# Spike counts summed by TensorE, two gather tiles, an eighth chunk held, and output tiles taken from the row buffers

## Chip, cores and metric

One core of a Trainium2 chip runs the whole program. The metric is the device time in microseconds (us) of one execution, as the median over many runs. 1 us is 1000 ns.

## What is computed

The inputs are 1024 sequences of 50 item numbers (`r_seq`), their lengths, and a table of 100001 embedding rows of 128 floats, whose row 0 counts as zero. For each time step the reference takes the running mean of the embeddings, normalises it over the batch, feeds it to a leaky integrate-and-fire neuron per sequence and feature, and averages the spikes over the 50 steps. The scores are the product of that average with the whole table: 1024 x 100001 floats, 409.6 MB.

```python
emb = emb_table.at[0].set(0.0)
e = emb[seq]
prefix = jnp.cumsum(e, axis=1)
denom = jnp.minimum(t_idx[None, :], lengths[:, None])
uF = prefix / denom[:, :, None]
y = (uF - uF.mean(0)) * lax.rsqrt(uF.var(0) + BN_EPS) * gamma + beta
def step(v, x):
    v = v + (x - v) / TAU
    spike = atan_spike(v - V_TH)
    v = v - spike * V_TH
    return v, spike
_, spikes = lax.scan(step, v0, x_seq)      # 50 steps
scores = spikes.mean(axis=0) @ emb.T
```

## The kernel before

The program has two stages. Instructions stand in every engine's queue in the order in which the Python code issues them (line 49 switches any reordering off), so a wait in a queue holds all that is behind it.

**Stage one, the 50 steps** (loop of line 271). Everything is held transposed, features on the 128 partitions and the 1024 sequences along the row, in two halves of 512. For each step POOL (GpSimd) issues 8 indirect DMAs (line 187), one for each block of 128 sequences, that fetch the embeddings of that step into a tile `e`. There are three such tiles (`gather`, line 166), and the gather of step t+1 is issued at the head of step t, so it can run ahead until it needs a tile whose readers are not done. PE (TensorE) adds the prefix sum up in PSUM: `pre[0]` and `pre[1]`, one for each half, get 8 transposing matmuls out of `e` (line 284) and a matmul each that takes out row 0 (`correct`, line 252). DVE (VectorE) then reads `pre` into `uF` (line 293), half by half, and takes batch statistics (lines 294 and 298). The second half of `uF` can't start before the last four of the 8 transposes. Still on DVE come the spikes of the step before, `s` (line 308, 1 or 0 in bf16), and five small operations that make the scale `a` (lines 310 to 316). ACT (ScalarE) makes the square root and two passes over the whole row (lines 302, 303 and 322). DVE ends the step with `negv` (line 330), the new potential `v` (line 325, in PSUM, tiles `v0` and `v1` in turn), and `count` (line 263): it adds the step's spikes to a running sum in SBUF. The next transposes stand in PE's queue directly behind `correct`, and `correct` needs `uF` of the step to be read.

At steps 42, 44 and 46, and at the end, a quarter (1024 rows) of the first chunk of the table is prepared as well (`prepare`, line 138): 8 transposes on PE into a PSUM tile `pt`, a copy on ACT that rounds to the upper part `hi` (line 132), and a subtraction on DVE for the rest, `lo` (line 136).

**Stage two, the product** (loop of line 391). The table is cut into 25 chunks of 4096 rows; the last has 1697. `AHEAD = 7` chunks are loaded at the very start on SP's queue (line 180), the others in stage two on ACT's queue, one after each chunk. The prepared quarters live in six pairs of tiles `hi` and `lo`, taken in turn (`slot`, line 105). For each of the 8 blocks of 128 sequences, PE multiplies the four quarters by the counts (`product`, line 145, two parts in two banks for each quarter), DVE and ACT in turn scale the result into an output tile `o` (lines 403 and 405; three tiles of 16 KB a partition), and SP's queue stores it (line 157, 2 MB). The four quarters of the next chunk are prepared after the third block, after the sixth, and two inside the last block (lines 409 to 414).

Of the kernel before, what the change touches and what calls it, by code (L numbers as in the profile page):

```python
# [12 lines left out]
F32 = mybir.dt.float32  # L13
BF16 = mybir.dt.bfloat16
F32R = mybir.dt.float32r
# [5 lines left out]
P = 128  # L21
BN_EPS = 1e-5
V_TH = 1.0
CH = 4096
AHEAD = 7
HALF = 1024
KQ = HALF // P
BANK = 512
# [3 lines left out]
def rec_kernel(  # L32
# [17 lines left out]

    const = ctx.enter_context(tc.tile_pool(name="const", bufs=1))
    embp = ctx.enter_context(tc.tile_pool(name="embT", bufs=1))
    rowp = ctx.enter_context(tc.tile_pool(name="rows", bufs=AHEAD - 1))


    countA = const.tile([P, P], F32R, tag="countA", name="countA")
# [9 lines left out]
    chunks = [(c0, min(CH, N - c0)) for c0 in range(0, N, CH)]  # L66
    rows = {}
    split = {}
    order = {}
    for c, (c0, w) in enumerate(chunks):  # L70
        for q in range(-(-w // HALF)):
            order[c, q] = len(order)

    def fetch(c, pool):

# [27 lines left out]
            nc.tensor.transpose(pt[:, k0 : k0 + kw], rows[c][:kw, q * KQ + k0 // P, :], ident[:kw, :kw])  # L103

    def slot(c, q):
        i = order[c, q] % 6
        pool = embp if i < 4 else embp2
        hi = pool.tile([P, HALF], F32R, tag=f"hi{i}", name=f"hi_{c}_{q}")
        lo = pool.tile([P, HALF], F32R, tag=f"lo{i}", name=f"lo_{c}_{q}")
        split[c, q] = hi, lo  # L110
        return hi, lo

    def views(c, q, pt, hi, lo):
# [18 lines left out]
        nc.scalar.copy(vh, vp)  # L132

    def lower(c, q, pt):
        vp, vh, vl = views(c, q, pt, *split[c, q])
        nc.vector.tensor_tensor(vl, vp, vh.bitcast(F32), ALU.subtract)  # L136

    def prepare(c, q, pt):
# [5 lines left out]

    def product(po, c, q, n, k0, kw):
        kw += kw % 2
        for j, part in enumerate(split[c, q]):
# [12 lines left out]
    with ExitStack() as ph:  # L160
# [2 lines left out]
        lp = ph.enter_context(tc.tile_pool(name="lif", bufs=2))  # L163
        sp = ph.enter_context(tc.tile_pool(name="stats", bufs=3))
        up = ph.enter_context(tc.tile_pool(name="uF", bufs=2))
        gp = ph.enter_context(tc.tile_pool(name="gather", bufs=3))
        accp = ph.enter_context(tc.tile_pool(name="acc", bufs=1, space=bass.MemoryType.PSUM))
        vp = ph.enter_context(tc.tile_pool(name="v", bufs=1, space=bass.MemoryType.PSUM))

# [74 lines left out]
        def only(t):  # L244

# [4 lines left out]
        def correct(t, l):  # L250
            for h in range(B // BANK):
                nc.tensor.matmul(  # L252
                    pre[h],
                    lhsT=l,
                    rhs=zT[:, h * BANK : (h + 1) * BANK],
                    start=t == 0,
                    stop=False,
                    skip_group_check=True,
                )


        def spiked(out, cs, v):
            nc.vector.scalar_tensor_tensor(out, v[:, cs], V_TH, count[:, cs], ALU.is_ge, ALU.add)  # L263
# [7 lines left out]
        for t in range(T):  # L271
            last = t == T - 1
            if t + 1 < T:
                gather(t + 1)
            e = es.pop(t)
            if last:
                s = lp.tile([P, B], BF16, tag="s", name=f"s_{t - 1}")
                nc.vector.tensor_single_scalar(s, v, V_TH, ALU.is_ge)
                nc.vector.tensor_tensor(negv, s, v, ALU.subtract)
            uF = up.tile([P, B], F32, tag="uF", name=f"uF_{t}")  # L280
            bs = sp.tile([P, B // BANK, 6], F32, tag="bs", name=f"bs_{t}")
            for h, cs in enumerate(halves):
                for k in range(0, BANK, P):
                    nc.tensor.matmul(  # L284
                        pre[h][:, k : k + P],
                        lhsT=e[:, h * BANK + k : h * BANK + k + P],
                        rhs=ident,
                        start=False,
                        stop=last,
                        is_transpose=True,  # L290
                        skip_group_check=True,
                    )
                nc.vector.scalar_tensor_tensor(uF[:, cs], rlen[:, cs], 1.0 / (t + 1), pre[h], ALU.max, ALU.mult)  # L293
# [12 lines left out]
            if t and not last:  # L306
                s = lp.tile([P, B], BF16, tag="s", name=f"s_{t - 1}")
                nc.vector.tensor_single_scalar(s, v, V_TH, ALU.is_ge)  # L308
# [12 lines left out]
            def x(cs):  # L321
                nc.scalar.activation(vt[:, cs], uF[:, cs], AF.Identity, bias=hgb[:, 1:2], scale=a)  # L322

            def step(cs):
                nc.vector.scalar_tensor_tensor(vt[:, cs], negv[:, cs], -0.5, vt[:, cs], ALU.mult, ALU.add)  # L325

            if not last:
                x(whole)
                if t:
                    nc.vector.tensor_tensor(negv, s, v, ALU.subtract)  # L330
                step(whole)
                v = vt
# [11 lines left out]
        pt = accp.tile([P, HALF], F32, tag="pt", name="pt_3")  # L344
# [18 lines left out]
        spiked(countB, slice(P, BANK), vt)  # L363
        spiked(countC, halves[1], vt)
        for q in range(1, 4):
            o = (up if q == 3 else gp).tile([P, HALF], F32, tag="uF" if q == 3 else "e", name=f"o_0_0_{q}")
            po = (accp if q % 2 == 0 else vp).tile(
                [P, HALF], F32, tag="v0" if q % 2 else "pt", name=f"po_0_0_{q}"
            )
            for k0 in range(0, HALF, BANK):  # L370
                product(po[:, k0 : k0 + BANK], 0, q, 0, k0, BANK)
            for h, cs in enumerate(halves):
                if h == 0:
                    nc.scalar.mul(o[:, cs], po[:, cs], 1.0 / T)
                else:
                    nc.vector.tensor_scalar_mul(o[:, cs], po[:, cs], 1.0 / T)
# [10 lines left out]
    def ready(c, q):  # L387
        if (c, q) in order:
            prepare(c, q, psum.tile([P, HALF], F32, tag="ps", name=f"pt_{c}_{q}"))

    for c, (c0, w) in enumerate(chunks):
        for n in range(NB):
            if c == 0 and n == 0:
                continue
            o = op.tile([P, CH], F32, tag="o", name=f"o_{c}_{n}")
            for q in range(-(-w // HALF)):
# [21 lines left out]

# [17 lines left out]
```

## Time and profile before

| what | value |
|---|---|
| median of 14 runs | 1677.32 us (1676.72 to 1678.48) |
| the profiled execution: its time | 1679.74 us |
| its span, first to last instruction | 1678.0 us |
| the rest of that time, around the span | 1.74 us |
| POOL's first and last gather | begins at 3.91 us, ends at 567.44 us |
| `uF` of the last step begins | 591.12 us |
| first store of scores issued | 600.18 us |
| busy over the span | PE 1054.0, DVE 999.3, ACT 630.7, POOL 379.2 us |
| read from and written to memory | 77.69 MB and 409.60 MB |

The span is the time from the first to the last instruction of the profiled execution. A group of instructions is a line of the kernel on one engine with one kind of operation; its row gives the busy time in all, the mean of one, and how long the engine stood idle just before it and what ended that. "remote" is put where the profile knows no sender of the signal that ended a wait. Starts of matmuls are recorded, their ends are modelled, and some records of them can be missing.

### The profile page before, as it was taken

Reading aid. Unit: us, or ns where it says so; the run is one execution under the profiler, and the core shown is the slowest. Engines: PE = TensorE matmul, PEld = TensorE weight load, DVE = VectorE, ACT = ScalarE, POOL = GpSimd, SP = SyncE. Lnnn points to the kernel's source line nnn. Section 1 sums busy time; section 2 is a strip of 40 time slices with the busy share of each in tenths; the row PEclk is TensorE's granted clock in tenths of the full one; section 3 lists DMA queues with packets and bytes.
Section 4 is the critical chain, followed back from the end, with each engine's and each line's share of the span. In section 5 each row is a group of like instructions: output and inputs, shape, how many; then the busy total and the mean of one; then the engine's idle time right before and its main releaser. Section 6 shows DMA issues by size and latency. Waiting matters only on the chain.

```text
span 1678.0 us, 12554 instructions
## 1 busy us (share of the span) xinstructions
PE 1054.0 (63%) x4434; PEld 804.0 (48%) x4434; DVE 999.3 (60%) x1211; ACT 630.7 (38%) x697; POOL 379.2 (23%) x406
## 2 busy tenths in 40 slices
PE   3223323232223378778878788777877888888886
PEld 2112212221112256666666566656666666666664
DVE  5577767777768775555555455544555555555553
ACT  2122222222223244444444344444444444444452
POOL 7666666666667300000000000000000000000000
PEclk7555555555555589999999999999999999999998
DMA  9311111111111169999999999999999999999998
GB/s 342 104 46 49 48 44 47 47 46 46 46 45 49 27 255 418 425 425 421 425 418 418 415 416 419 419 425 412 418 416 419 415 424 422 417 411 413 418 413 352
DMA packets 58411, 488.14 MB, mean 291 GB/s; under 512 B 12491, under 2 KB 13292, under 8 KB 33772
## 3 DMA queue, kind: packets, MB, share of 16 engines
q1 hardware_dynamic: 35728, 424.57, 60.1%
q0 software_dynamic: 12800, 26.24, 6.0%
q10 hardware_dynamic: 9820, 36.52, 6.0%
q8 instruction: 35, 0.57, 0.1%
q14 instruction: 28, 0.23, 0.0%
HBM read 77.69 MB, written 409.60 MB: 290 GB/s over the span
## 4 chain that ended last, share of the span: by engine, by line
DMA 49%; DVE 29%; PE 7%; another core or an unknown queue 7%; issue 4%; ACT 3%; DVEq 0%; SPq 0%; ACTq 0%; POOLq 0%
DMA scores<-o 48%; PE po L148 6%; DVE o L403 6%; DVE bs L294 4%; DVE uF L293 4%; DVE v L325 3%; DVE count L263 3%; DVE s L308 3%; DVE negv L330 2%; ACT o L405 2%; ACT v L322 1%; DVE a L316 1%; DMA e<-in_L_rec_emb_table,idx 1%; DVE mv L298 1%
## 5 line engine op out<-in xcount | busy, mean ns | idle before, releaser
L403 DVE TENSOR_SCALAR o<-po 128x1024 f32<-128x1024 f32 x390 | 462.2, 1220 | 442.9 <-DMA scores<-o 357.5
L405 ACT ACTIVATE o<-po 128x1024 f32<-128x1024 f32 (+1 forms) x390 | 385.6, 1018 | 546.6 <-DMA scores<-o 382.7
L187 POOL DMA_INDIRECT e<-in_L_rec_emb_table,idx x400 | 378.5, 946 | 187.6 <-issue 114.0
L148 PE MATMUL po<-hi,countC 128*128 128x512 f32 x784 | 332.0, 424 | 91.8 <-ACT o L405 91.1
L252 PE MATMUL pre<-zT,l 128*128 128x512 f32 x100 | 77.3, 775 | 386.3 <-DVE uF L293 313.8
L148 PE MATMUL po<-lo,countC 128*128 128x512 f32 x784 | 317.7, 406 | 0.0
L148 PE MATMUL po<-hi,countB 128*128 128x512 f32 x588 | 243.2, 414 | 32.0 <-ACT o L405 31.5
L148 PE MATMUL po<-lo,countB 128*128 128x512 f32 x588 | 235.8, 401 | 0.0
L252 PEld LDWEIGHTS pre<-zT,l 128*128 128x128 f32 x100 | 28.7, 288 | 428.2 <-issue 313.5
L148 PEld LDWEIGHTS po<-hi,countC 128*128 128x128 f32 x784 | 154.5, 197 | 154.8 <-ACT o L405 124.4
L148 PEld LDWEIGHTS po<-lo,countC 128*128 128x128 f32 x784 | 154.7, 197 | 29.3
L103 PE MATMUL pt<-ident,rows 128*128 128x128 f32 x782 | 113.5, 292 | 74.2 <-ACT o L405 68.0
L302 ACT ACTIVATE r<-mv,eps 128x1 f32<-128x1 f32 x50 | 14.7, 295 | 386.6 <-DVE mv L298 229.9
L136 DVE TENSOR_TENSOR lo<-pt,hi 128x1024 fp32r<-128x1024 f32 x98 | 117.4, 1216 | 63.3 <-ACT hi L132 63.3
L148 PEld LDWEIGHTS po<-hi,countB 128*128 128x128 f32 x588 | 115.5, 196 | 69.8 <-ACT o L405 41.5
L103 PEld LDWEIGHTS pt<-ident,rows 128*128 128x128 f32 x782 | 96.6, 150 | 98.6 <-ACT o L405 83.6
L293 DVE SCALAR_TENSOR_TENSOR uF<-rlen,pre 128x512 f32<-128x512 f32 x100 | 67.8, 678 | 122.8 <-remote 105.5
L148 PEld LDWEIGHTS po<-lo,countB 128*128 128x128 f32 x588 | 115.2, 196 | 22.7
L132 ACT CAST hi<-pt 128x1024 fp32r<-128x1024 f32 x98 | 98.9, 1010 | 55.9 <-PE pt L103 42.8
L284 PE MATMUL pre<-ident,e 128*128 128x128 f32 x400 | 98.6, 419 | 11.0 <-DMA e<-in_L_rec_emb_table,idx 8.4
L284 PEld LDWEIGHTS pre<-ident,e 128*128 128x128 f32 x400 | 83.5, 220 | 24.3 <-issue 12.4
L148 PE MATMUL po<-hi,countA 128*128 128x512 f32 x194 | 76.0, 392 | 1.6 <-ACT o L405 1.1
(61 smaller groups left out, 678.5 us busy)
## 6 DMA issues: line engine op xcount, KB each, us to landing
scores<-o SPq DMA_DIRECT2D x190, 2048.0 KB
rows<-in_L_rec_emb_table ACTq DMA_DIRECT2D x17, 2048.0 KB
rows<-in_L_rec_emb_table SPq DMA_DIRECT2D x7, 2048.0 KB
scores<-o SPq DMA_DIRECT2D x8, 848.5 KB
e<-in_L_rec_emb_table,idx POOLq DMA_INDIRECT x400
scores<-o SPq DMA_DIRECT2D x2, 1024.0 KB
scores<-o SPq DMA_DIRECT2D x3, 512.0 KB
scores<-o SPq DMA_DIRECT2D x2, 256.0 KB
```

The lines of the kernel that those rows point to most:

```text
L103: nc.tensor.transpose(pt[:, k0 : k0 + kw], rows[c][:kw, q * KQ + k0 // P, :], ident[:kw, :kw])
L132: nc.scalar.copy(vh, vp)
L136: nc.vector.tensor_tensor(vl, vp, vh.bitcast(F32), ALU.subtract)
L148: nc.tensor.matmul(po[:, :kw], lhsT=counts[n], rhs=part[:, k0 : k0 + kw], start=j == 0, stop=j == 1,)
L187: nc.gpsimd.indirect_dma_start(out=es[t][:, n * P : (n + 1) * P], out_offset=None, in_=table, in_offset=bass.IndirectOffsetOnAxis(ap=idx[: ...
L252: nc.tensor.matmul(pre[h], lhsT=l, rhs=zT[:, h * BANK : (h + 1) * BANK], start=t == 0, stop=False, skip_group_check=True,)
L263: nc.vector.scalar_tensor_tensor(out, v[:, cs], V_TH, count[:, cs], ALU.is_ge, ALU.add)
L284: nc.tensor.matmul(pre[h][:, k : k + P], lhsT=e[:, h * BANK + k : h * BANK + k + P], rhs=ident, start=False, stop=last, is_transpose=True, ...
L293: nc.vector.scalar_tensor_tensor(uF[:, cs], rlen[:, cs], 1.0 / (t + 1), pre[h], ALU.max, ALU.mult)
L294: nc.vector.bn_stats(bs[:, h, :], uF[:, cs])
L403: nc.vector.tensor_scalar_mul(o[:, h0 : h0 + hw], po[:, :hw], 1.0 / T)
L405: nc.scalar.mul(o[:, h0 : h0 + hw], po[:, :hw], 1.0 / T)
```

## The change

Six things change together.

- The running sum `count` on DVE is gone from the steps. A new function `counted` lets PE add the spikes `s` of step t-1 into two more PSUM banks, `sums`, by two bf16 matmuls with an identity. It is called in step t right after `s`, so in PE's queue it stands between `correct` and the next step's transposes. In the last step two ACT copies bring `sums` into SBUF, in the tile of `zT`.
- The gather has two tiles in place of three.
- `AHEAD` is 8: an eighth chunk is loaded at the start, into a tile of its own (`extra`). The number of row tiles stays 6.
- Prepared quarters take a pair of tiles from a list of free ones, and a pair is free again when its last product is issued. There are five pairs until chunk 7 (the one in `extra`) is prepared; then its tile serves as two more pairs. With five, one quarter of the next chunk is prepared after the third block and three inside the last one.
- The quarters prepared within the steps go through the PSUM tile `v1` or `v0` in place of a `pt` of their own, and the first product uses `sums`.
- The outputs of the last chunk go to row tiles (six of them) in place of the three tiles `o`.

```diff
-AHEAD = 7
+AHEAD = 8
-    rowp = ctx.enter_context(tc.tile_pool(name="rows", bufs=AHEAD - 1))
+    rowp = ctx.enter_context(tc.tile_pool(name="rows", bufs=AHEAD - 2))
+    extrap = ctx.enter_context(tc.tile_pool(name="extra", bufs=1))
...
+    free = [(embp, i) for i in range(4)]
...
     def slot(c, q):
-        i = order[c, q] % 6
-        pool = embp if i < 4 else embp2
+        place = free.pop(0)
+        pool, i = place
+        if pool is None:
+            hi, lo = i
...
-        gp = ph.enter_context(tc.tile_pool(name="gather", bufs=3))
+        gp = ph.enter_context(tc.tile_pool(name="gather", bufs=2))
...
-            fetch(c, rowp if c else row0p)
+            fetch(c, row0p if c == 0 else extrap if c == AHEAD - 1 else rowp)
...
-        count = once.tile([P, B], F32, tag="count", name="count")
-        nc.vector.memset(count, 0.0)
+        ident_h = once.tile([P, P], BF16, tag="ident_h", name="ident_h")
+        nc.vector.tensor_copy(ident_h, ident)
...
+        sums = [accp.tile([P, BANK], F32, tag=f"sums{h}", name=f"sums{h}") for h in range(B // BANK)]
...
+        def counted(t, s):
+            for h in range(B // BANK):
+                nc.tensor.matmul(
+                    sums[h],
+                    lhsT=ident_h,
+                    rhs=s[:, h * BANK : (h + 1) * BANK],
+                    start=t == 0,
+                    stop=t == T - 2,
+                    skip_group_check=True,
+                )
...
             if not last:
                 correct(t + 1, l)
+            else:
+                counted(t - 1, s)
+                count = once.tile([P, B], F32, tag="zT", name="count")
+                for h, cs in enumerate(halves):
+                    nc.scalar.copy(count[:, cs], sums[h])
...
             if t and not last:
                 s = lp.tile([P, B], BF16, tag="s", name=f"s_{t - 1}")
                 nc.vector.tensor_single_scalar(s, v, V_TH, ALU.is_ge)
+                counted(t - 1, s)
...
-                if t < T - 2:
-                    spiked(count, whole, v)
...
-                    prepare(0, q, accp.tile([P, HALF], F32, tag="pt", name=f"pt_{q}"))
+                    prepare(0, q, vp.tile([P, HALF], F32, tag="v1", name=f"pt_{q}"))
...
-        spiked(count, whole, v)
...
+    free.append((embp2, 4))
     turn = 0
+    ahead = list(range(AHEAD, len(chunks)))
...
+        todo = [(c + 1, q) for q in range(parts[c + 1])] if c + 1 < len(chunks) else []
+        def ready():
+            if todo and free:
+                i, q = todo.pop(0)
+                prepare(i, q, psum.tile([P, HALF], F32, tag="ps", name=f"pt_{i}_{q}"))
...
-            o = op.tile([P, CH], F32, tag="o", name=f"o_{c}_{n}")
+            if c + 1 < len(chunks):
+                o = op.tile([P, CH], F32, tag="o", name=f"o_{c}_{n}")
+            else:
+                o = rowp.tile([P, CH], F32, tag="rows", name=f"o_{c}_{n}")
...
-                if n == NB - 1 and q < 2:
-                    ready(c + 1, 2 + q)
+                if n == NB - 1:
+                    free.append(split.pop((c, q))[2])
+                    ready()
...
             if n in (2, 5):
-                ready(c + 1, n // 5)
-        if c + AHEAD < len(chunks):
-            fetch(c + AHEAD, rowp)
+                ready()
+        if c + 2 == AHEAD:
+            more = extrap.tile([P, 4, HALF], F32R, tag="rows", name="more")
+            free += [(None, (more[:, i, :], more[:, i + 1, :])) for i in (0, 2)]
+        elif ahead:
+            fetch(ahead.pop(0), rowp)
```

More of the change, by code (lines that the diff above doesn't have):

```diff
@@ L68, in rec_kernel @@
     split = {}
[L69 to L72, printed above, removed]
+    parts = [-(-w // HALF) for _, w in chunks]
+    free = [(embp, i) for i in range(4)]
     def fetch(c, pool):
@@ L105, in slot @@
     def slot(c, q):
-        i = order[c, q] % 6
-        pool = embp if i < 4 else embp2
-        hi = pool.tile([P, HALF], F32R, tag=f"hi{i}", name=f"hi_{c}_{q}")
-        lo = pool.tile([P, HALF], F32R, tag=f"lo{i}", name=f"lo_{c}_{q}")
-        split[c, q] = hi, lo
+        place = free.pop(0)
[3 more added lines that the diff above has]
+        else:
+            hi = pool.tile([P, HALF], F32R, tag=f"hi{i}", name=f"hi_{c}_{q}")
+            lo = pool.tile([P, HALF], F32R, tag=f"lo{i}", name=f"lo_{c}_{q}")
+        split[c, q] = hi, lo, place
         return hi, lo
@@ L134, in lower @@
     def lower(c, q, pt):
-        vp, vh, vl = views(c, q, pt, *split[c, q])
+        vp, vh, vl = views(c, q, pt, *split[c, q][:2])
         nc.vector.tensor_tensor(vl, vp, vh.bitcast(F32), ALU.subtract)
@@ L146, in product @@
         kw += kw % 2
-        for j, part in enumerate(split[c, q]):
+        for j, part in enumerate(split[c, q][:2]):
             nc.tensor.matmul(
@@ L339, in rec_kernel @@
                     q = (t - T + 8) // 2
-                    prepare(0, q, accp.tile([P, HALF], F32, tag="pt", name=f"pt_{q}"))
-        pt = accp.tile([P, HALF], F32, tag="pt", name="pt_3")
+                    prepare(0, q, vp.tile([P, HALF], F32, tag="v1", name=f"pt_{q}"))
+        pt = vp.tile([P, HALF], F32, tag="v0", name="pt_3")
         turned(0, 3, pt)
@@ L365, in rec_kernel @@
         for q in range(1, 4):
[L366 to L371, printed above, removed]
+            pool, tag = (gp, "e") if q == 1 else (up, "uF")
+            o = pool.tile([P, HALF], F32, tag=tag, name=f"o_0_0_{q}")
+            if q == 1:
+                po = sums
+            else:
+                po = vp.tile([P, HALF], F32, tag=f"v{(q + 1) % 2}", name=f"po_0_0_{q}")
+                po = [po[:, cs] for cs in halves]
             for h, cs in enumerate(halves):
[L373 to L376, printed above, removed]
+                product(po[h], 0, q, 0, h * BANK, BANK)
+            nc.scalar.mul(o[:, :BANK], po[0], 1.0 / T)
+            nc.vector.tensor_scalar_mul(o[:, BANK:], po[1], 1.0 / T)
             store(0, q * HALF, o)
@@ L384, in rec_kernel @@
     )
+    free.append((embp2, 4))
     turn = 0
-    def ready(c, q):
-        if (c, q) in order:
-            prepare(c, q, psum.tile([P, HALF], F32, tag="ps", name=f"pt_{c}_{q}"))
+    ahead = list(range(AHEAD, len(chunks)))
     for c, (c0, w) in enumerate(chunks):
+        todo = [(c + 1, q) for q in range(parts[c + 1])] if c + 1 < len(chunks) else []
[3 more added lines that the diff above has]
+                prepare(i, q, psum.tile([P, HALF], F32, tag="ps", name=f"pt_{i}_{q}"))
         for n in range(NB):
@@ L394, in rec_kernel @@
                 continue
-            o = op.tile([P, CH], F32, tag="o", name=f"o_{c}_{n}")
-            for q in range(-(-w // HALF)):
+            if c + 1 < len(chunks):
+                o = op.tile([P, CH], F32, tag="o", name=f"o_{c}_{n}")
+            else:
+                o = rowp.tile([P, CH], F32, tag="rows", name=f"o_{c}_{n}")
+            for q in range(parts[c]):
                 h0 = q * HALF
@@ L413, in rec_kernel @@
             if n in (2, 5):
-                ready(c + 1, n // 5)
-        if c + AHEAD < len(chunks):
-            fetch(c + AHEAD, rowp)
+                ready()
+        assert not todo
+        if c + 2 == AHEAD:
[3 more added lines that the diff above has]
+            fetch(ahead.pop(0), rowp)
 _INS = ["r_seq", "r_lengths", "L0_rec_emb_table", "L0_rec_gamma", "L0_rec_beta"]
```

## The prediction

> **What bounds the kernel now.** I read the page's totals and its strips of slices first, then stretches of stage two, then the groups and waits of the steps, and last the timeline of two steps. The first two show two stages with different limits.
>
> ```profile
> span 1678.0 us, 12554 instructions
> DMA  9311111111111169999999999999999999999998
> ...
> 1200.00:1400.00 200.00, 162.10 (x714) 126.25 (x712) 103.17 (x88) 87.98 (x89) 0.00 (x0) 0.95 1.01 420
> 1655.00:1660.00 5.00, 3.02 (x8) 2.27 (x8) 1.21 (x2) 0.72 (x2) 0.00 (x0) 0.59 0.71 284
> 1660.00:1665.00 5.00, 4.39 (x11) 3.59 (x12) 3.17 (x3) 2.02 (x3) 0.00 (x0) 0.50 0.67 272
> ```
>
> Each digit of the strip is 42 us. From about 600 us the DMA engines are full: in the stretch 1200 to 1400 their share is 1.01 (last but one column) at 420 GB/s, with PE busy 162 of 200 us. Stage two is bytes over rate. Near its end, from 1655 to 1665, the share falls to 0.71 and 0.67. Before 600 us transfers bound nothing, and the steps are read from their waits:
>
> ```profile
> L187 POOL DMA_INDIRECT e<-in_L_rec_emb_table,idx x400 | 378.5, 946 | 187.6 <-issue 114.0 <-remote 62.2 <-PE pre L252 6.9
> L263 DVE SCALAR_TENSOR_TENSOR count<-v,count 128x1024 f32<-128x1024 f32 x49 | 60.0, 1224 | 1.9
> L252 PE MATMUL pre<-zT,l 128*128 128x512 f32 x100 | 77.3, 775 | 386.3 <-DVE uF L293 313.8 <-issue 52.7 <-DVE count L263 15.4
> ...
> DVE uF L293 <- remote: 105.5, 23, 8.4
> POOL e L187 <- remote: 62.2, 17, 5.6
> POOL e L187 <- PE pre L252: 6.9, 2, 3.7
> ```
>
> POOL issues a gather in 0.946 us and pauses 0.30 before the next, so a round of 8 takes 10.0 us, and 50 rounds 500 of the 563.5 us from its first gather to the end of its last. The rest is 19 waits, 62.2 + 6.9 = 69.1 us, 3.64 each. DVE waits 105.5 us in 23 waits ahead of `uF`. So the steps are paced by POOL's rounds and by these waits, not by DVE's work. The timeline shows what they wait for:
>
> ```profile
> 150.14 0.69 DVE L293 SCALAR_TENSOR_TENSOR uF<-rlen,pre 128x512 f32<-128x512 f32 x1 [6.52 <-remote]
> 150.38 0.94 POOL L187 DMA_INDIRECT e<-in_L_rec_emb_table,idx  x1 [3.66 <-remote]
> ...
> 151.48 1.91 PE L284 MATMUL pre<-ident,e 128*128 128x128 f32 x8
> ...
> 151.72 1.17 DVE L308 TENSOR_SCALAR s<-v 128x1024 bf16<-128x1024 f32 x1
> ...
> 158.91 0.67 DVE L293 SCALAR_TENSOR_TENSOR uF<-rlen,pre 128x512 f32<-128x512 f32 x1
> ...
> 160.23 1.91 PE L284 MATMUL pre<-ident,e 128*128 128x128 f32 x8
> ...
> 167.25 0.69 DVE L293 SCALAR_TENSOR_TENSOR uF<-rlen,pre 128x512 f32<-128x512 f32 x1 [0.84 <-remote]
> ...
> 169.14 0.94 POOL L187 DMA_INDIRECT e<-in_L_rec_emb_table,idx  x1 [0.30 <-issue]
> 173.59 0.69 DVE L293 SCALAR_TENSOR_TENSOR uF<-rlen,pre 128x512 f32<-128x512 f32 x1 [4.91 <-remote]
> 173.82 0.94 POOL L187 DMA_INDIRECT e<-in_L_rec_emb_table,idx  x1 [3.74 <-remote]
> ```
>
> Transposes that begin at 160.23 are over at 162.14, yet the `uF` that reads them waits until 167.25 and, for its second half, until 173.59. POOL, waiting for the same tile to come free, restarts 0.23 us after that. So PE's work is done, but the signal that says so is late. The semaphore updates in the trace agree: PE's counter steps every 1.4 to 3.5 us from 153.7 to 173.5, while gathers flow, then three times within 0.07 us, 3.5 us after POOL's last gather ended. The transposes of 151.48, by contrast, began 1.1 us after POOL had restarted, before the new gathers' first packets (152.1 us), and both halves of their `uF` (157.59 and 158.91) start without any wait. A step without a wait is 158.91 - 150.14 = 8.77 us. PE's signals are thus prompt only while no gather flows; otherwise they come at the latest 2 to 5 us after POOL stops. That is my reading; the sender itself is not named.
>
> **The change, part by part.**
>
> *PE's counts and their place.* `counted` stands ahead of the next transposes and waits for `s`. In the view `s` ends at 152.89. Two bf16 matmuls of 512 columns are not in the trace: the nearest rows are 0.42 us (a 128x128 f32 transpose) and 0.775 (512 columns of `correct`). I take 0.775, as the columns are the same: 1.55 us. Transposes that began at 151.48 then begin at 152.89 + 1.55 = 154.4 (153.7 at the low end), end at 156.4, and fall wholly into the flow of gathers. As PE time alone, 48 x 1.55 = 74 us (low end 40) cost nothing: PE is busy about 57 of every 200 us of the steps; with that cover gone they would cost all of it. What is queued behind `counted` is just these transposes; `uF` and POOL's tile wait for them.
>
> The Trainium skill (TensorE: Matmul & The Clock Gate, section "Wait — 56ns, not 53.3ns?") has a 512-column matmul every 426.7 ns on a cold array; the granted clock is 0.50 in the steps here. By it the pair is an estimated 0.85 us, and the transposes begin at 153.7: still in the flow.
>
> *Two tiles.* After a wait POOL now has one landed tile in hand and one to fill. It can only go on without a wait if the tile in hand is answered for within the 9.7 us of its round. With transposes that start in the flow, I expect the answer only after POOL stops. So rounds 2 to 49, 48 of them, each wait 3.64 us, where 19 do now. A wait takes the place of a 0.30 pause: (48 - 19) x 3.34 = **+96.9**. Ends for a wait: the three rounds that now follow a wait with another wait took 13.45, 12.72 and 13.50 us, so 3.0 to 3.8, or 48 x 2.7 - 63.4 = +66 to 48 x 3.5 - 63.4 = +105. At the end there is a gain: now two steps follow POOL's last wait (567.44 to the last `uF` at 591.12 is 23.7 us); with two tiles only one does, 3.64 + 8.77 - 1.22 = 11.2: **-12.5**.
>
> The Trainium skill (SBUF — State Buffer, section "SBUF: two separate sides") says that PE never waits on any other port user and that DMA and compute can't slow each other. By that rule the transposes' place would not matter and this part would cost 0. The rows have PE unhindered too (8 transposes in 1.91 us), but the reader 5 to 11 us late, and I go by the rows.
>
> *DVE's running sum.* 49 x 1.224 = 60 us of work go, the step without waits falls to 7.55. **0** on the path: POOL's round of 10.0 us is longer than either. With that cover gone it would be -60. The sum at the very end (1.22 at 595.42) lies under ACT's two passes until 597.19: 0. The two ACT copies that come in (0.6 each by the row of line 374) run while `uF` and its statistics take 2.8 us: 0, at most +1.2.
>
> *The eighth chunk.* 2.10 MB less to read in stage two, at 420 GB/s: **-5.0**. At the start the same 2.10 MB are loaded more, at 388 GB/s (20 to 40 us) 5.4 us: 0 to +5.4. I take 0, since from 53 us on POOL waits for answers anyhow, and SP's queue, which issues it, has nothing behind it until 600 us.
>
> *Last outputs.* From 1655 to 1665 DMA loses 10 x (1 - 0.69) = 3.1 us, as DVE and ACT wait for a tile `o` to be stored. Six row tiles take that wait away: **-3**, ends 0 and -3.1.
>
> *Five pairs, quarters through `v1`.* One preparation of six chunks moves into the last block: 8 transposes x 0.292, 1.01 on ACT, 1.22 on DVE, 4.6 us if nothing overlaps. Two stores of 2.10 MB (5.0 us each) are queued then: 0, at most 6 x 4.6 = +28 with that cover gone, nearer 0. The transposes into `v1` now wait for `negv`, and `lo` on DVE for them, up to 1.8 us three times: 0 to +5.4, under POOL's wait: 0. The change of a PSUM tile alone: 0.
>
> Sum: 96.9 - 12.5 - 5.0 - 3.0 = +76.4. The profiled execution took 1679.74 (span 1678.0 and 1.74 around it), 2.42 above the median. 1679.74 + 76.4 - 2.42 = **1753.7**, say 1754. Its own range, with +66 to +105 for the waits and the small upper ends (+5.4, +1.2, +5.4), is 1723 to 1774.
>
> **Rivals.**
>
> 1. *Waits as often as today.* The answers come within POOL's round of 9.7 us even for the later transposes, so the steps keep their pace and only -5 and -3 remain: 1677.3 - 8 = 1669, not slower. For: the transposes of 151.48 were answered by 157.6 and 158.9. Against: those of 160.23 took 13.4 us. It decides from an answer 9.7 us after POOL's restart.
> 2. *DVE's share is real.* If DVE's 1.22 us come off every step, 1677.3 - 60 - 8 = 1609; POOL's rounds without any wait give about the same, -63.4 - 8, 1606. For: the chain of waits gives 3% of the span to `count`. Against: 10.0 us of POOL a round.
> 3. *Two tiles, one wait in two rounds.* 24 waits in place of 19: 5 x 3.34 = +17, or +8 with the gains: 1686; with two in three, 32 waits, +43 - 8 gives 1712.
> 4. *Nothing to see.* The load at the start gives back what the read saves, and the tail's 3.1 us is filled otherwise: 1677.
>
> **How the numbers follow.** Every round waits 0.60, rival 3 0.13, rival 1 0.12, rival 2 0.11, rival 4 0.04. A measurement here can tell about 0.2%, 3.4 us, from no change: faster 0.23 (rivals 1 and 2), same 0.04, slower 0.73. The likeliest case gives 1754. The range reaches down over rival 3 to rival 1, and up to waits of 4 us (48 x 3.7 - 63.4 = +114, 1771) with the small upper ends: 1664 to 1780. Below it lies rival 2.
>
> **What would show it.** In the profile of the changed kernel: POOL's waits ahead of a gather number about 47 and sum to some 170 us; its last gather ends near 660; `uF` begins 13 to 14 us apart, with a wait nearly every time; `counted` sits ahead of the transposes, which begin 3 to 4 us after POOL's restart; DVE has 60 us less work and more idle time; stage two is 8 us shorter, with a period of 40 us rather than 45 in chunk 6 and no dip before the end. I am wrong if the transposes that follow `counted` are answered while gathers still flow, which shows as rounds of 10.0 us without a wait, or if stage two loses its full DMA share in the last blocks of chunks 0 to 5.

## The result, and the profile after

The changed kernel took 1660.4 us (median of 6 runs, 1659.8 to 1662.7) beside 1677.1 of the kernel before (28 runs): a ratio of 0.9903 [0.9893, 0.9913], 16.7 us less. The forecast was 1754. The profiled execution took 1659.77 us, its span 1658.0. First the page's totals and strips, then three groups with their idle time, then three rows of the waits (us in total, times, longest):

```profile
span 1658.0 us, 12678 instructions
DMA  9411111111111189999999999999999999999998
```

```profile
L191 POOL DMA_INDIRECT e<-in_L_rec_emb_table,idx x400 | 378.6, 947 | 188.5 <-issue 115.6 <-remote 64.8 <-PE pre L257 4.3
L257 PE MATMUL pre<-zT,l 128*128 128x512 f32 x100 | 74.4, 746 | 247.9 <-DVE uF L309 196.5 <-issue 41.2 <-DVE v L348 8.9
L268 PE MATMUL sums<-s,ident_h 128*128 128x512 bf16 x87 | 44.9, 606 | 64.2 <-issue 36.6 <-DVE s L330 25.5 <-DVE s L294 2.1
```

```profile
DVE uF L309 <- remote: 134.6, 26, 10.6
POOL e L191 <- remote: 64.8, 16, 5.6
POOL e L191 <- PE pre L257: 4.3, 1, 4.3
```

POOL waits 17 times, 64.8 + 4.3 = 69.1 us in sum. Before it was 19 times, and 69.1 us too. The number of tiles, PE's queue and DVE's work all changed, and the sum did not. POOL's last gather ends at 568.48 (567.44 before), so a gather takes 1.41 us on average in both. The changed trace shows more: its 17 waits end one stretch of 32 gathers, 13 of 24 and 3 of 16, and last 5.6, 4.1 to 4.3, and 2.3 to 3.0 us. A wait thus grows with the number of gathers before it, by 0.14 to 0.19 us for each, and from restart to restart a gather takes 1.41 or 1.42 us in every stretch but the last (1.38). The rounds lie otherwise than before, as this stretch of the timeline shows (start, duration, engine, line, operation, idle time before it):

```profile
151.60 0.69 DVE L309 SCALAR_TENSOR_TENSOR uF<-rlen,pre 128x512 f32<-128x512 f32 x1 [3.52 <-remote]
151.84 0.95 POOL L191 DMA_INDIRECT e<-in_L_rec_emb_table,idx  x1 [4.27 <-remote]
...
154.40 1.01 PE L268 MATMUL sums<-s,ident_h 128*128 128x512 bf16 x2 [1.26 <-DVE s L330]
...
155.21 1.91 PE L300 MATMUL pre<-ident,e 128*128 128x128 f32 x8
...
157.77 0.68 DVE L309 SCALAR_TENSOR_TENSOR uF<-rlen,pre 128x512 f32<-128x512 f32 x1
...
162.69 1.92 PE L300 MATMUL pre<-ident,e 128*128 128x128 f32 x8 [0.22 <-issue]
...
164.35 0.95 POOL L191 DMA_INDIRECT e<-in_L_rec_emb_table,idx  x1 [0.30 <-issue]
165.26 0.68 DVE L309 SCALAR_TENSOR_TENSOR uF<-rlen,pre 128x512 f32<-128x512 f32 x1
...
181.33 0.69 DVE L309 SCALAR_TENSOR_TENSOR uF<-rlen,pre 128x512 f32<-128x512 f32 x1 [8.49 <-remote]
...
185.59 0.69 DVE L309 SCALAR_TENSOR_TENSOR uF<-rlen,pre 128x512 f32<-128x512 f32 x1 [2.85 <-remote]
185.83 0.95 POOL L191 DMA_INDIRECT e<-in_L_rec_emb_table,idx  x1 [4.26 <-remote]
```

POOL restarts at 151.84. Transposes that begin 3.4 us and 10.9 us later, in the middle of the flow, are answered at once (`uF` at 157.77 and 165.26, no wait). Only the third step's answer is late. POOL then restarts at 185.83: three rounds in 34.0 us, that is 24 gathers at 1.417 us each, although POOL issued all 24 at one each 1.25 and only then waited.

Where the 20.0 us of span went, from start times in the two traces (the medians are only 16.7 apart: the profiled execution of before lay 2.6 above its median, the changed one 0.6 below, so some 3 us of these differences belong to the two executions):

| | before | after | difference |
|---|---|---|---|
| last gather ends | 567.44 | 568.48 | +1.0 |
| from there to the last step's `uF` | 23.7 | 6.2 | -17.4 |
| from there to the first store | 9.1 | 9.1 | 0 |
| from the first store to the end of the span | 1077.8 | 1074.2 | -3.6 |

In the last row, the period that ends with chunk 7's last store fell from 45.2 to 40.1 us, and those of chunks 0 and 1 grew by 0.5 and 0.4. The tail, in windows of the changed kernel (length, PE, PEld, DVE, ACT, POOL busy, clock, DMA share, GB/s), has no dip any more:

```profile
1645.00:1650.00 5.00, 0.00 (x0) 0.00 (x0) 0.56 (x1) 0.05 (x1) 0.00 (x0) 0.50 1.01 410
1650.00:1655.00 5.00, 0.00 (x0) 0.00 (x0) 0.00 (x0) 0.00 (x0) 0.00 (x0) 0.50 0.28 113
```

Yet nothing is gained there: from the issue of chunk 23's last store to the last packet it is 29.2 us in both kernels. From 1652 to 1656 the share is 0.05 to 0.10, about one engine of 16: a single DMA engine still moves its packets of 6788 bytes, 0.265 us each, back to back, after the others are done. The last store is issued 12.4 us before the end of the span now, in place of 6.1 (at 1645.6 of 1658.0; before, at 1671.9 of 1678.0), but the slowest engine sets the end.

### The profile page after: what moved, and what is told of

It reads as the page before. It is cut to its first block, busy times and chain, and to the rows that moved or that the text cites. A ratio compares the mean times of both kernels' runs of the same rounds, so it can differ in the third digit from the quotient of the medians.

```text
span 1658.0 us, 12678 instructions
## 1 busy us (share of the span) xinstructions
PE 1096.1 (66%) x4521; PEld 812.6 (49%) x4532; DVE 938.4 (57%) x1162; ACT 632.0 (38%) x699; POOL 379.3 (23%) x406
## 4 chain that ended last, share of the span: by engine, by line
DMA 46%; DVE 25%; PE 10%; another core or an unknown queue 9%; issue 4%; ACT 4%; DVEq 0%; ACTq 0%; SPq 0%
DMA scores<-o 46%; PE po L152 8%; DVE o L434 5%; DVE bs L310 4%; DVE uF L309 4%; DVE v L348 3%; DVE s L330 3%; ACT o L436 3%; DVE negv L353 2%; ACT v L345 1%; PE pt L104 1%; DVE a L339 1%; DVE mv L320 1%; DVE q L336 0%
## 5 line engine op out<-in xcount | busy, mean ns | idle before, releaser
L152 PE MATMUL po<-hi,countC 128*128 128x512 f32 x624 | 261.7, 419 | 81.1 <-ACT o L436 80.9
L152 PE MATMUL po<-lo,countC 128*128 128x512 f32 x624 | 250.0, 401 | 0.0
L152 PE MATMUL po<-hi,countB 128*128 128x512 f32 x468 | 192.9, 412 | 14.1 <-ACT o L436 13.6
L152 PE MATMUL po<-lo,countB 128*128 128x512 f32 x468 | 188.0, 402 | 0.0
L152 PEld LDWEIGHTS po<-hi,countC 128*128 128x128 f32 x624 | 120.9, 194 | 132.2 <-ACT o L436 109.3
L324 ACT ACTIVATE r<-mv,eps 128x1 f32<-128x1 f32 x50 | 14.7, 295 | 375.5 <-DVE mv L320 254.3
L152 PEld LDWEIGHTS po<-lo,countC 128*128 128x128 f32 x624 | 121.2, 194 | 22.5
L140 DVE TENSOR_TENSOR lo<-pt,hi 128x1024 fp32r<-128x1024 f32 x78 | 93.8, 1219 | 39.5 <-ACT hi L136 36.1
L152 PEld LDWEIGHTS po<-hi,countB 128*128 128x128 f32 x468 | 91.6, 196 | 41.8 <-ACT o L436 19.4
L152 PEld LDWEIGHTS po<-lo,countB 128*128 128x128 f32 x468 | 91.5, 196 | 18.3
L152 PE MATMUL po<-more,countC 128*128 128x512 f32 (+1 forms) x320 | 85.0, 404 | 15.9 <-ACT o L436 15.9
```

What stands on the lines that cost most here:

```text
L152: nc.tensor.matmul(po[:, :kw], lhsT=counts[n], rhs=part[:, k0 : k0 + kw], start=j == 0, stop=j == 1,)
```

## The experiments

The sets of runs went to different chips, and the kernel before was measured in each: 1671.0 us in the first set, 1593.8 in the second, 1677.6 in the third, 1593.3 in the fourth, 1671.7 in the fifth. Each set is compared with its own.

**Two tiles alone, the rest without them, both.** Three kernels of the first set: the kernel before with two gather tiles (and one more output in a tile of `uF`, so that it fits); the changed kernel with seven chunks and three tiles, which has the counts on PE and the smaller parts; the changed kernel with seven chunks.

```diff
 (before)  -gp = ... bufs=3     +gp = ... bufs=2
 (after)   -AHEAD = 8           +AHEAD = 7,  gather bufs=3
 (after)   -AHEAD = 8           +AHEAD = 7
```

> The kernel before with two gather tiles in place of three (and the output of quarter 2 in a uF tile), nothing else. Theory F (a floor on gathers): 400 gathers are served at 1.41 us each in the long run, whatever the number of tiles; POOL's last gather ends at 567 +/- 4 us, its waits still sum to about 69 us, and only the lag from there to the last uF shrinks from 23.7 us to 9 to 14, so the time falls by 9 to 15 us, to 1662 to 1668. Theory T (waits are made by tiles that are answered for late, as the prediction had it): 40 or more waits of 3.6 us, POOL's end near 630 or later, time 1720 to 1770.

> The changed kernel with three gather tiles again, and seven chunks held so that it fits (the seventh in the extra tile). The read costs 5.0 us against the changed kernel. Theory F: POOL's end is unchanged at 568 +/- 4; the steps are 7.5 us, so the lag to the last uF lies between the changed kernel's 6 us and 20 us; time 1665 to 1680. Theory T: three tiles in place of two save waits, POOL's end is earlier by 10 us or more and the time is below 1660.

> The changed kernel with seven chunks held in place of eight, nothing else. One read of 2.1 MB more in stage two: +5.0 us if the DMA engines are the bound of stage two throughout (1665.4), and none of it in stage one; 0 if the read would be hidden. The load at the start is shorter by 2.1 MB: if that load delays the first rounds, up to 5 us come back and the sum is near 0.

Measured: 1665.1 us, ratio 0.9966 [0.9950, 0.9981]; 1673.4, 1.0014 [1.0004, 1.0024]; 1663.0, 0.9957 [0.9943, 0.9971]. Two tiles alone bring 5.9 us where the forecast's step made them cost tens; theory F had 9 to 15 for them. In the three traces a gather takes 1.399, 1.400 and 1.407 us on average. Their waits, in this order (two rows for the first):

```profile
POOL e L187 <- remote: 55.9, 14, 5.5
POOL e L187 <- PE pre L252: 8.2, 2, 5.5
POOL e L191 <- remote: 67.3, 21, 6.5
POOL e L191 <- remote: 69.2, 19, 5.4
```

The sums are 64.1, 67.3 and 69.2 us. What differs is the lag from the end of the last gather to the last step's `uF`: 12.5, 17.4 and 6.3 us. Within this set, going from three tiles to two in the changed kernel (the second against the third) takes 11.1 us off the lag and 10.4 off the time. In the kernel before, two tiles take 5.9 off the time; its lag here is not known, for its only trace, with 23.7, comes from another set, in which it was 6.1 us slower. With two tiles already there, the counts on PE and the rest shorten the lag by another 6.2, but the last gather ends 3.0 later in that execution (566.55 and 563.59), and the time falls by 2.1. From the first store to the last packet of a store the three take 1076.6, 1077.1 and 1077.2 us; the changed kernel with its eighth chunk, 1072.6 in the first measurement. The eighth chunk was not tried alone within one set.

**A floor under the gathers?** From here on theory F: the stage is held to one gather each 1.41 us whatever the waits are, and a wait only pays back what the issue at 1.25 ran ahead. A small memset on POOL behind each gather, the spacer, slows the issue.

```diff
+        spare = once.tile([P, 64], F32, tag="spare", name="spare")
         (in gather, behind each indirect_dma_start)
+                nc.gpsimd.memset(spare, 0.0)
```

> The changed kernel with a small POOL memset (128x64) behind every gather, so that POOL issues them every 1.35 to 1.5 us rather than every 1.25. Theory F (served at 1.41 us each): nothing is lost as long as the spacing is at most 1.41: POOL's end stays at 568 to 572, while its waits for tiles, and DVE's late starts of uF, all but vanish; time 1658 to 1665. Theory T: the waits stay at some 4 us in three rounds and the spacing comes on top, 400 x 0.1 to 0.25 = 40 to 100 us, time 1700 to 1760.

Measured: 1659.7 us, 0.9944 [0.9927, 0.9961]. The issue slowed only to 1.28 us. POOL's waits, now in part ahead of the memset:

```profile
POOL e L192 <- remote: 40.2, 17, 3.7
POOL e L192 <- PE pre L259: 3.1, 1, 3.1
POOL spare L198 <- remote: 8.8, 10, 1.5
```

They fell from 69.2 (seven chunks) to 52.1 in sum, and the last gather ended 2.7 us later. That leans to F but is too small a change to tell.

**The same with more space, and with half of the gathers (second set).** Memsets of 128x192 and 128x384, the changed kernel itself, and a kernel that leaves out half of the gathers.

```diff
-            for n in range(NB):
+            for n in range(0, NB, 2):
 (and the transposes of an odd block read the even one beside it)
```

> The changed kernel itself, so that the next runs have it as their neighbour on one chip. Both theories expect the ratio to the kernel before that it had, 0.990, give or take 0.002: about 16 to 17 us less.

> The changed kernel with a memset of 128x192 on POOL behind each gather, 0.25 to 0.27 us by the 0.165 of 128x64 and the 0.205 of 128x128, so that POOL issues a gather each 1.37 to 1.40 us where it is free, in place of 1.25. Theory F (the stage is held to one gather each 1.41 us whatever the waits; a wait only pays back what the issue ran ahead): the waits shrink from 69 us to some 5 to 15, POOL's last gather still ends at 565 to 575, the time is that of the changed kernel, give or take 3 us. Rival W (a wait is a price of its own, paid so and so often, and the rounds' own length comes on top): 400 x 0.13 = 52 us more on the rounds, and waits as now: 40 to 52 us slower than the changed kernel.

> The same with a memset of 128x384, 0.40 to 0.43 us, so that POOL issues a gather each 1.51 to 1.56 us. Theory F: now the issue is slower than the floor of 1.41; nothing runs ahead, so no waits at all (under 10 us in sum), stage one lasts 400 x (1.51 to 1.56) = 604 to 624 in place of 564: 40 to 60 us slower than the changed kernel. Rival W: 400 x 0.28 = 112 us more on the rounds with waits as now: 100 to 112 us slower.

> The changed kernel with only the even four of a step's eight gathers; an odd block of sequences takes the embeddings of the even one beside it, so half of the gathers is left out and all work behind them stays. Theory F: 200 gathers x 1.41 = 282 us is under the 50 steps of DVE's own (7.49 each, 375 us), so DVE's steps set stage one: some 180 to 195 us less than the changed kernel, POOL waiting for tiles each step, and PE's signals prompt all along. Rival W2 (late signals come with gathers in flight as such): steps of 11 us would stay for a good part, and the gain would be under 120 us.

Measured: 1589.3 us, 0.9973 [0.9962, 0.9984]; 1647.0, 1.0335; 1709.9, 1.0728; 1479.6, 0.9284. F missed all four numbers: the change is worth 4.4 us, the spacers cost their full 58 and 121 us (its rival had 52 and 112 for the longer rounds), and half of the gathers saves 110. But there are no waits at all, and with half of the gathers the steps take the 7.48 us that F gave them. The changed kernel's own trace says why; rows of its waits, then of the timeline:

```profile
POOL e L191 <- issue: 117.9, 387, 0.3
DVE uF L309 <- PE pre L300: 105.9, 46, 3.1
```

```profile
154.48 0.48 PE L300 MATMUL pre<-ident,e 128*128 128x128 f32 x1 [0.74 <-DMA e<-in_L_rec_emb_table,idx]
155.61 0.94 POOL L191 DMA_INDIRECT e<-in_L_rec_emb_table,idx  x1 [0.30 <-issue]
155.71 0.47 PE L300 MATMUL pre<-ident,e 128*128 128x128 f32 x1 [0.75 <-DMA e<-in_L_rec_emb_table,idx]
...
156.22 0.69 DVE L309 SCALAR_TENSOR_TENSOR uF<-rlen,pre 128x512 f32<-128x512 f32 x1 [2.45 <-PE pre L300]
```

Behind its first gather POOL has not one wait over 0.6 us: rounds of 10.0 us from first to last, the last gather ends at 504.0, PE turns each block as it lands, and `uF` follows the last transpose of its half by 0.04 us in about half of the cases (here from 155.71 + 0.47 to 156.22), in the flow. No signal is late.

**The four again (third set).** Theory C: the floor and the late signals belong to the chip or the place on it, not to the kernel.

> The changed kernel again, on whatever chip it falls to. Theory C (PE's late done-signals, and with them the 69 us of waits, belong to the chip: two chips have them, the third, where the kernel before takes 1594 us, has none): where the kernel before takes 1670 to 1680, POOL's waits are 60 to 75 us in sum and the change is worth 11 to 18 us; where it takes about 1594, no waits and 4 to 5 us. Rival R (the third chip's run without waits was one of several paces that a start may fall into on any chip): executions of both kinds among the rounds of one chip, 70 to 80 us apart.

> The changed kernel with the memset of 128x192 behind each gather, which slowed it by 58 us where there were no waits (a gather each 1.39 us in place of 1.25). On a chip with waits, theory F (there the stage is held to one gather each 1.41 us, the waits only pay back what the issue ran ahead) expects the waits to shrink from 69 us to under 15 and the time to stay that of the changed kernel within 5 us. Rival W (a wait is a price of its own) expects waits as now and 40 to 58 us more.

> The same with the memset of 128x384 (a gather each 1.55 us, 120 us slower where there were no waits). On a chip with waits, theory F: slower than the floor, so the waits go to nearly nothing and the time is that of the chip without waits, about 1710 us: some 50 us more than the changed kernel. Rival W: waits as now and 100 to 120 us more.

> The changed kernel with only the even four of a step's eight gathers, an odd block taking the even one's embeddings, so that half of the gathers is left out. 1480 us where there were no waits, a step each 7.49 us, set by DVE. On a chip with waits, theory F: four gathers in 7.49 us are 1.87 us each, slower than the floor of 1.41, so nothing is late and the time is 1480 there too, within 10 us. Rival W2 (late signals come with gathers in flight, as such): steps of 9 to 11 us for a good part, 1520 us or more.

Measured: 1660.8 us, 0.9903 [0.9887, 0.9920]; 1662.7, 0.9917 [0.9900, 0.9933]; 1710.8, 1.0197; 1479.1, 0.8816. POOL's groups, in this order:

```profile
L191 POOL DMA_INDIRECT e<-in_L_rec_emb_table,idx x400 | 377.6, 944 | 191.1 <-issue 113.7 <-remote 72.1 <-DMA idx<-in_r_seq 2.9
```

```profile
L192 POOL DMA_INDIRECT e<-in_L_rec_emb_table,idx x400 | 381.5, 954 | 83.4 <-issue 65.8 <-remote 14.7 <-DMA idx<-in_r_seq 2.7
L198 POOL MEMSET spare<- 128x192 f32 x400 | 110.6, 276 | 0.3
```

```profile
L192 POOL DMA_INDIRECT e<-in_L_rec_emb_table,idx x400 | 381.5, 954 | 69.4 <-issue 59.7 <-PE pre L302 6.9 <-DMA idx<-in_r_seq 2.9
L198 POOL MEMSET spare<- 128x384 f32 x400 | 174.5, 436 | 0.3
```

The waits are back ("remote" 72.1), and now F holds with room: the memset that cost 58 us where there were no waits costs 1.9 us here, because the waits fall to 14.7. The last gather ends 5.8 us later (575.88 and 570.07), and the lag behind it is 5.4 us shorter. With the larger memset the issue is slower than the floor (1.55 us a gather), no wait is left, and the time is that of the set without waits (1710.8 and 1709.9). With half of the gathers it is the same too (1479.1 and 1479.6, a step each 7.48 us). The rival, a wait as a price of its own, wanted 40 to 58 us more for the first spacer. That several paces mix on one chip was not seen: within each set the kernel before stays within 0.4%.

**Last outputs, half of the rows, the spacer in the kernel before (fourth and fifth sets).** The last chunk's outputs back in the tiles `o`; all 400 gathers for 64 of their 128 sequences, which leaves out half of the rows; the memset of 128x192 in the kernel before.

```diff
-            if c + 1 < len(chunks):
+            if True:
...
-                    out=es[t][:, n * P : (n + 1) * P],
+                    out=es[t][: P // 2, n * P : (n + 1) * P],
 (idx and the transposes likewise)
```

> The changed kernel as neighbour for the next three. On a chip with waits a ratio of 0.990 to the kernel before (16 to 17 us), on one without 0.997 (4 to 5 us).

> The changed kernel with the last chunk's outputs in the three output tiles again, as before. The prediction's term for the tiles of the rows was -3 us (so this would be 3 us slower than the changed kernel). By the traces, where the end lies 29.2 us behind the issue of the last full chunk's last store in both kernels because the slowest DMA engine sets it, it is 0, within 1 us.

> The changed kernel with all 400 gathers, but each for the first 64 of its 128 sequences: half of the rows is left out, and the transposes turn 64 columns each. On a chip with waits, theory G (the floor of 1.41 us is the gather's, as an instruction): stage one stays at 564 us, or at 400 gathers' issue if that is longer, with waits: within 10 us of the changed kernel's time there, 1660. Theory D (the floor goes by the rows or their descriptors): 0.71 us for each, so issue or DVE's steps of 7.49 set the stage, no waits, 1480 to 1590 us, and the same on every chip.

> The kernel before with the memset of 128x192 behind each gather (a gather each 1.39 us in place of 1.25). On a chip with waits, theory F: the waits fall from 69 us to under 25, the time stays that of the kernel before or falls by up to 15 us (less lag behind the last gather). Rival W, the reading on which the prediction stood (a late signal costs 3.64 us, 19 times): rounds longer by 400 x 0.14 = 56 us, waits as now, 45 to 56 us slower. On a chip without waits both expect 45 to 60 us more.

> The changed kernel with all 400 gathers, each for the first 64 of its 128 sequences only: half of the rows is left out, and the transposes turn 64 columns each. Where there were no waits it took 1574 us, a gather each 1.21 us. Where there are waits (the kernel before 1670 to 1680): theory G (the floor of 1.41 us is the gather's, as an instruction): stage one as long as the changed kernel's there, waits of 70 to 85 us, 1650 to 1665 us. Theory D (the floor goes by the rows or their descriptors, 0.71 us a gather here): no waits, 1574 us, within 5.

> The kernel before with the memset of 128x192 behind each gather; 57 us slower where there were no waits. Where there are waits, theory F: they fall from 69 us to under 25, and the time is that of the kernel before or up to 15 us less. Rival W (the prediction's reading, a late signal costs 3.64 us, 19 times, on top of the rounds): 45 to 57 us slower.

Measured in the fourth set, where there were no waits (although its chip bore the same number as the third's): 1589.1 us, 0.9973 [0.9964, 0.9983]; 1589.0, 0.9975 [0.9965, 0.9985]; 1573.6, 0.9877; 1650.7, 1.0361. The last outputs are worth nothing, in either tile: 0.0 us apart. The other two can't tell the theories apart without waits, so they were run again.

Measured in the fifth, with waits: half of the rows 1658.9 us, 0.9925 [0.9901, 0.9949]; the kernel before with the spacer 1669.9, 1.0004 [0.9986, 1.0023]. POOL's groups of these two:

```profile
L191 POOL DMA_INDIRECT e<-in_L_rec_emb_table,idx x400 | 362.4, 906 | 203.9 <-issue 109.6 <-remote 43.0 <-PE pre L257 41.6
```

```profile
L188 POOL DMA_INDIRECT e<-in_L_rec_emb_table,idx x400 | 380.6, 951 | 74.6 <-issue 66.5 <-remote 4.8 <-DMA idx<-in_r_seq 3.0
L194 POOL MEMSET spare<- 128x192 f32 x400 | 110.2, 276 | 3.5 <-remote 2.6 <-POOL spare L194 0.4 <-issue 0.2
```

With half of the rows POOL is done sooner with each gather (0.906) and waits longer (43.0 + 41.6 = 84.6): a gather still takes 1.41 us, and stage one is as long as ever. The floor goes by the gather, not by its rows. In the kernel before, the memset that cost 57 us in the fourth set costs nothing: the same floor held it. Its waits ("remote" in the two rows) are 4.8 + 2.6 = 7.4 us in sum, where its first profile had 69.1.

With the whole computation no run was clearly faster than the changed kernel, by its ratio to the kernel before of the same set.

## Why the prediction was wrong, step by step

**The step that failed** is the one that read a price into the waits: "With transposes that start in the flow, I expect the answer only after POOL stops. So rounds 2 to 49, 48 of them, each wait 3.64 us, where 19 do now", +96.9 us. Measured: 17 waits, 69.1 us, +0. Transposes at 155.21 and 162.69 start in the flow and are answered at once. The runs put a floor in its place: where there are waits, the stage takes 1.40 to 1.43 us a gather with two tiles or three, with counts on DVE or PE, and with an issue slowed from 1.25 to 1.39. The waits only fill up 50 rounds of 10.0 us to 400 times 1.41 = 564. The prediction had both numbers, 500 us of rounds and 563.5 of stage, divided the difference by 19, and took the quotient for a price that could be counted again. That the same sum could be shared by any number of waits was not asked. Its rival 1 (waits as often as today, 1669) is what came, short by the lag at the end; the answers within the round, on which rival 1 rested, came in two rounds of three. To the rounds from which the step took the two ends of its price, 13.45, 12.72 and 13.50 us, the trace has a fourth, of 14.16 us, behind a wait of 0.8: the price was not constant even there.

- *Rounds of 10.0 us*: right, 9.7 of issue and a pause of 0.30.
- *Counts on PE*: the transposes do begin 3.4 us after POOL's restart (3 to 4 forecast), and PE's time is free; the pair takes 1.01 us by its modelled end, and the transposes start 0.81 behind its start, where 1.55 was taken. The estimate of 0.85 by the Trainium skill (TensorE: Matmul & The Clock Gate, section "Wait — 56ns, not 53.3ns?") was nearer.
- *The place of the transposes*: the rule weighed against it (the Trainium skill, SBUF — State Buffer, section "SBUF: two separate sides") made this part 0, and 0 it was, but by luck and not by the rule's reason: signals are late behind gathers here (the `uF` at 181.33 starts late, after 8.49 us of idle time, though all its step's transposes were over by 173.7), and the part is 0 because the floor takes up the waits. The rows that were preferred to the rule were sound; the price read out of them was not.
- *Gain at the end, -12.5*: the mechanism was right and the size short, -17.4 between the two traces. In the first set two tiles take 11.1 us off the lag, and with two tiles the counts on PE and the rest take off 6.2; that the 6.2 are the shorter step of DVE, which was put at 0 on the path, is the likely reading, not a tested one. POOL's rounds and the floor hid DVE's 60 us everywhere else.
- *DVE's running sum*: 0 elsewhere, right. Busy time fell by 61 us (999.3 to 938.4), and without the two tiles and the eighth chunk the changed kernel was 2.4 us slower than the kernel before.
- *Eighth chunk, -5.0*: the period that ends with chunk 7's last store is 5.1 shorter (the prediction looked for it in chunk 6); 0.9 came back in the first two. Where there are no waits this is about all that the change brings. With the memset of 128x192 in both kernels the first store is at 570.7 (before, fourth set) and 571.4 (changed, second set), and from there to the last packet 1076.2 and 1071.7.
- *Last outputs, -3*: 0, by the trace and by the run. The dip was real, but the slowest DMA engine, not the dip, set the end.
- *Load at the start, five pairs, quarters through `v1`*: 0 each, as put; the last gather ends 1.0 later, and no later period of stage two is over 0.6 longer.

With the wait term at 0 the forecast's other terms make -20.5, or 1656.8. So one term lost the sign. That 1656.8 lies near the measured 1660.4 is in part luck: the gain at the end was put 4.9 too small and the last outputs 3 too large. The range ended at 1664, by its rival 1, and left the time out. (Its upper end adds up to 1783, not 1780: 1771 and small ends of 12.)

## What to carry to other kernels

When a wait ends a stretch of work that ran ahead, add up the stretch and the wait, over many of them, before you price the wait: if rate times count gives the stage, the waits are its remainder, and moving them is worth nothing. The cheap test is to slow the issuer a little; if the time stays, there is a floor below it, and what still counts is the lag behind its last item. And a floor found on one chip may be absent on the next, so measure both kernels side by side in every set.

## What the runs showed of the hardware

- In three of five sets, and in the first measurement, 128-row gathers back to back on POOL go through at 1.40 to 1.43 us each although POOL issues one each 1.25; in two sets they go at 1.25. The kernel before is 1671 to 1678 us on the one kind and 1593 to 1594 on the other. The number of the chip does not tell them apart.
- The floor is not the transfer of the rows: in the packet records of the two first traces a gather's packets start 0.70 to 0.74 us after its issue ends, all through a run of gathers (from 55 us on, when the loads of the start are over), and the DMA share is 0.18. Halving the rows leaves it. What stayed the same there is the gather itself and its 32 packets, 16 with data (4096 bytes each, 2048 with half of the rows) and 16 of 4 bytes. The Trainium skill (DMA: Bandwidth & Descriptors, section "Why a DMA increments its semaphore by 16 and not by 1") says that all 16 engines post their own increment for a DMA from POOL whatever its shape, which fits the 16 small packets. Whether these, the descriptors or something else makes the floor was not tried. Every execution on record has the span and clock that a profile gives, so no run shows whether the floor is there without one either.
- Where there is a floor, PE's signals come late behind gathers. In the stretch of the changed kernel shown above, those of PE's semaphore updates that are on record are prompt for the first 13 gathers after the restart (164.40, 166.57 and 167.83 us, each within 0.02 of the end of a matmul) and late at the end: the last transposes are over by 173.7, and the last updates come at 185.50 to 185.61, 3.9 us after POOL's last gather ended. The 13 is no rule: in the kernel before, transposes that were over at 162.14, some 10 gathers after a restart, were answered at 167.25. Why PE's signals should be held up by gathers is open; that they are late only behind such a backlog is what the larger spacer and the half of the gathers show.
- The record of semaphore updates itself differs between the two kinds of sets. The eight semaphores of the gathers have 1325 updates on record in the changed kernel's first trace and 1153 in that of the kernel before, where 16 for each of 400 gathers would be 6400; in the second and fourth sets the changed kernel has 6397 and 6400. With the larger memset, in the set with waits, it is 6148. Whether the missing ones were merged on the chip or lost by the record is not known. The prediction read PE's counter from such a record ("steps every 1.4 to 3.5 us"), so only the late starts of `uF` carry that reading.
